# Query scaling on ScalarE, finer VectorE steps, moved loads and scatters, and expert pages in a written order, in a two-layer attention and mixture-of-experts kernel

## The chip, the cores and the metric

The kernel runs on one core of a Trainium2 chip. The core has five engines that run side by side, each with its own queue of instructions: TensorE (PE: matmuls and transposes; its weight loads are listed as PEld), VectorE (DVE), ScalarE (ACT), GpSimd (POOL), and SyncE (SP), which here only issues DMAs. POOL and ACT issue DMAs as well; the indirect ones (gathers and scatters by a list of rows) are issued by POOL. Engines wait for each other through semaphores, and an engine starts its instructions strictly in the order of its queue.

The metric is the device time of one execution in microseconds, smaller is better. An execution is taken as its span, from first to last instruction, and a small rest around it.

## The reference, cut to what matters

The input x is [4, 256, 256] in float32: 1,024 tokens of width 256. Four sublayers follow one another, each as x = x + layernorm(f(layernorm(x))).

```
# 1. attention over chunks of 32 tokens, 16 query heads, 4 key heads of 128
k = rms(xc @ w_k.T);  v = xc @ w_v.T;  q = rms(x @ w_q.T)        # rms over each head
scores = qr . landmark of each earlier chunk; 8 best; rw = softmax(scores)
p   = softmax over the 32 keys of each chosen chunk, times rw of the chunk
out = (p . v summed over chunks) @ w_o.T
# 2. mixture of 32 experts, 4 per token
logits = x @ gate_w.T + gate_b;  top 4, weights = softmax of the 4 logits
gate = min(xt @ w_gate + b_gate, 7);  up = clip(xt @ w_up + b_up, -7, 7)
o = ((up + 1) * gate * sigmoid(1.702 * gate)) @ w_down + b_down
y = sum over the 4 experts of o * weight
# 3. a gated scan over the 256 tokens of a row
lam = sigmoid(x @ W.T + b);  s = lam * s + (1 - lam) * x
# 4. a gated feed-forward layer with int8 weights, 256 -> 1024 -> 256
```

There are 8 chunks in a row of 256 tokens, so the best 8 are all the earlier chunks.

## The kernel before, in words

The program has three stages.

*Attention and routing* (us 0 to about 328 of the profile). The batch has four rows b of 256 tokens; a row is two tiles i of 128 tokens, so there are eight tiles. For each row the queries are made in 8 groups: a group is one tile and one key head kv, that is four query heads or 512 columns. One group goes: TensorE `pq` (L857); ScalarE squares each head and adds up (`jq`, L799, four instructions); VectorE `ssq` (L866) scales the sums; POOL `rq` (the helper `power`, L367) takes them to the power of minus one half; VectorE `qn` (L872) multiplies the four heads by it; TensorE turns them (`pqT`, L880), ScalarE copies them out (`qT`, L888). Keys go the same way (`pk` L808, `ssk` L814, `kn` L819, `pkT` L827, `kT` L831). Then come the scores (`s…` L957), a softmax per chunk in steps (`e…`: transpose and maximum on VectorE L900, subtraction on POOL L910, exponential on ScalarE L915, sums and inverse on VectorE, product), the products with v (`o…` L967, `att` L981) and the output matmul `wo` (L1005), one per tile.

Behind `wo` every tile is routed: the residual and two sets of statistics, the logits, the four best experts (`choose`), the rank of each token within its expert (`rank` L506), the slot (`rsl` L529) and the entries (`rent` L514) from which TensorE adds up the lists (`list` L539) that say which token stands in which row of which expert's page. From rank and expert VectorE also makes the rows (`places`) by which POOL scatters the normed token, once for each of its four experts, into `x_pages` in DRAM (L275): 32 scatters in all, four per tile.

The order of this stage is made when the program is built, by a list planner `Plan` (called `aplan`). Every step names its engine, an assumed cost, what it comes after, and the buffers that it takes and gives; a step whose chain to the end is the longest goes first, and a `lead` (LEAD for each later row) adds to the rank of the steps of the earlier rows. Steps named "D…" stand for the assumed arrival of loads (`arrival`). What the planner writes down is the order of instructions on every engine. At its end VectorE makes from the lists a gather list `gi` (L1115), and POOL's queue holds the scatters of tiles 4, 5 and 6, then the gathers, then the scatters of tile 7.

*Expert pages* (about 328 to 448). The 128 rows of one expert are a page; two pages go together (`pg` 0, 2 … 46: sixteen pairs for the 32 experts, then eight for rows that overflow a page). A pair goes: `page_fetch` (pages 0 to 7 by indirect gathers from `xn_dram` with gi, pages from 8 on read from x_pages by SP once all scatters have landed); `page_in` (transposes `px`, copy `pxT`); `page_up` (matmuls `pg` L1194 and L1199; VectorE `g` L1204 and `u` L1206; ScalarE sigmoid L1208; VectorE product L1209 and `h` L1211); `page_down` (transposes `ph` L1218, VectorE copy `hT` L1220, matmuls `po` L1224 and L1228, ScalarE copy `o` L1232, two scatters to `y_dram` by POOL, L1235). A `hook` adds side work between pairs: the lists of the overflow pages, the tables `mix` (L1406, L1408) for the sum over experts, the cast of the int8 weights (L1078). The order of instructions in this stage is left to the framework, which takes them as their inputs are due. The page's lists, weights and rows are read in `pages`, L1244 and on.

*Last layers* (448 to the end). `yk` (L1511) reads y_dram, TensorE sums the four experts with the tables mix (`y`, L1521), and the scan and the int8 layer follow under a second planner.

At the start POOL issues the loads of the gate and the biases (L331 to L338), fills the `att` tiles with zeros (L343), and then computes the small powers that the first tile waits for (L664 to L670, L367); SP issues x, the zero fill of x_pages and the expert weights.

## Time and profile before

| | us |
|---|---|
| median of 3 runs | 558.46 (557.94 to 558.66) |
| the profiled execution | 557.81 |
| its span | 556.0 |
| attention and the first seven tiles' routing, 16 to 285 | 269 |
| end of routing, 285 to 328 | 43 |
| pages, 328 to 448 | 120 |
| last layers, 448 to 556 | 108 |

The mean granted TensorE clock of the profiled execution is 0.934 of full speed. Its chain of work is 40% TensorE, 32% VectorE, 10% POOL, 7% issue, 5% ScalarE and 4% DMA.

The page gives the busy time of each engine over the whole span and then in slices; the table of stages gives the same for stretches that one chooses. A group line reads: source line, engine, operation, output and inputs by the program's names, shapes, count, then busy time, mean duration in ns, and the idle time of the engine just before these instructions with what ended it. A timeline line reads: start, duration, engine, source line, operation, and in brackets how long the engine had been idle before and what released it. Instructions of one engine overlap at their ends, so the distance from start to start is often shorter than the duration.

### The profile page before, as it was taken

The page shows a single profiled execution, that of the slowest core. Times are in us where ns is not written, and L with a number is a line of the kernel's source. Part 1 is how long each engine was busy: PE and PEld are TensorE (multiplying, and loading weights), DVE is VectorE, ACT ScalarE, POOL GpSimd, SP SyncE. Part 2 cuts the span into 40 slices and gives each one's busy share as a digit, 9 for nine tenths or more (in the row PEclk, how much of TensorE's full clock was granted, in tenths as well). Part 3 has the DMA queues.
Part 4 walks back from the last instruction along what each step waited for, and adds up shares of the span by engine and source line. Part 5 has one row for each costly group of instructions (what it writes and reads, how often), then busy time and mean ns, then how long its engine had stood idle before and what let it go on. Part 6 is the DMA issues. An engine that isn't in the chain of part 4 may idle for free.

```text
span 556.0 us, 7173 instructions
## 1 busy us (share of the span) xinstructions
PE 449.7 (81%) x1969; PEld 304.7 (55%) x1969; DVE 377.7 (68%) x1097; ACT 242.3 (44%) x762; POOL 313.0 (56%) x434
## 2 busy tenths in 40 slices
PE   0897988998979999888888227999999379589990
PEld 0353445664555565455666115888777258367760
DVE  3379997669897899999958944856444138853452
ACT  1674555534534545533220002336832117775541
POOL 6267676347446888436860774554554427845531
PEclk9999989999999999979999558999999879799996
DMA  8999999950000100003910584434957071000011
GB/s 255 360 386 369 349 348 348 349 189 1 9 1 21 38 10 28 2 28 99 365 57 9 161 308 129 131 118 145 367 175 243 23 260 45 1 0 1 1 40 38
DMA packets 59805, 80.68 MB, mean 145 GB/s; under 512 B 5684, under 2 KB 48682, under 8 KB 59760
## 3 DMA queue, kind: packets, MB, share of 16 engines
q1 hardware_dynamic: 54896, 70.33, 37.5%
q0 software_dynamic: 4576, 9.70, 5.1%
q10 hardware_dynamic: 288, 0.15, 0.2%
q8 instruction: 17, 0.28, 0.2%
q14 instruction: 28, 0.23, 0.1%
HBM read 37.16 MB, written 45.09 MB: 148 GB/s over the span
## 4 chain that ended last, share of the span: by engine, by line
PE 40%; DVE 32%; POOL 10%; issue 7%; ACT 5%; DMA 4%; another core or an unknown queue 1%; ACTq 0%; POOLq 0%; DVEq 0%; SPq 0%
PE pq L857 6%; PE pg L1199 5%; PE po L1228 3%; PE wo L1005 3%; PE y L1521 3%; PE u L1600 2%; PE d L1638 2%; PE g L1600 2%; POOL y_dram L1235 2%; PE pk L808 2%; DMA y_dram<-o,sib 1%; DMA gate_wT<-in_gate_wT 1%; PE px L1184 1%; DVE qn L872 1%; PE pqT L880 1%
## 5 line engine op out<-in xcount | busy, mean ns | idle before, releaser
L857 PE MATMUL pq<-w_q,xT 128*128 128x512 f32 x128 | 63.4, 619 | 3.6 <-DVE lm L733 1.3
L1005 PE MATMUL wo<-w_o,att 128*128 128x256 f32 x256 | 61.0, 382 | 3.9 <-DVE h L1025 3.9
L1005 PEld LDWEIGHTS wo<-w_o,att 128*128 128x128 f32 x256 | 47.3, 190 | 16.0 <-DVE h L1025 5.6
L1235 POOL DMA_INDIRECT y_dram<-o,sia x32 | 32.5, 1016 | 35.0 <-ACT o L1232 29.2
L799 ACT ACTIVATE jq<-pq 128x128 f32<-128x128 f32 x128 | 33.5, 275 | 28.3 <-PE pq L857 28.2
L367 POOL TENSOR_TENSOR rq<-ssq,mhalf 128x4 f32<-128x4 f32 x32 | 32.6, 1021 | 16.5 <-DVE ssq L866 16.1
L1204 DVE TENSOR_SCALAR g<-pg 128x256 f32<-128x256 f32 x24 | 10.2, 424 | 46.6 <-PE pg L1199 39.4
L857 PEld LDWEIGHTS pq<-w_q,xT 128*128 128x128 f32 x128 | 23.9, 197 | 27.4 <-issue 19.3
L275 POOL DMA_INDIRECT x_pages<-rxn,rowi x32 | 34.1, 1066 | 8.2 <-issue 6.8
L1199 PE MATMUL pg<-wexp,pxT 128*128 128x256 f32 x128 | 36.0, 395 | 0.2 <-issue 0.2
L1626 POOL TENSOR_TENSOR fl<-f,fh 128x512 fp32r<-128x512 f32 x15 | 19.2, 1290 | 23.4 <-ACT fh L1622 23.4
L1521 PE MATMUL y<-yk,mix 128*128 128x256 f32 x64 | 17.1, 417 | 11.9 <-DMA yk<-y_dram 11.2
L799 ACT ACTIVATION_READ_ACCUMULATOR jq<-pq 128x1 f32 x128 | 26.4, 206 | 0.0
L1232 ACT COPY o<-po 128x512 f32<-128x512 f32 x24 | 14.1, 585 | 27.4 <-PE po L1228 23.2
L1199 PEld LDWEIGHTS pg<-wexp,pxT 128*128 128x128 f32 x128 | 22.5, 198 | 4.3 <-issue 0.8
L1235 POOL DMA_INDIRECT y_dram<-o,sib x16 | 15.7, 984 | 16.0 <-ACT o L1232 13.2
L872 DVE TENSOR_TENSOR qn<-pq,rq 128x512 f32<-128x512 f32 x32 | 21.8, 680 | 4.2 <-POOL rq L367 2.3
L1615 DVE SCALAR_TENSOR_TENSOR f<-u,cols,sg 128x512 f32<-128x512 f32 x16 | 12.0, 750 | 18.4 <-PE u L1600 10.7
L888 ACT COPY qT<-pqT 128x512 f32<-128x512 f32 x32 | 18.8, 586 | 11.1 <-PE pqT L880 11.0
L880 PE MATMUL pqT<-ident,qn 128*128 128x128 f32 x128 | 20.2, 281 | 2.8 <-ACT qT L888 1.9
L880 PEld LDWEIGHTS pqT<-ident,qn 128*128 128x128 f32 x128 | 15.6, 146 | 10.4 <-issue 4.7
L1521 PEld LDWEIGHTS y<-yk,mix 128*128 128x128 f32 x64 | 12.9, 209 | 15.1 <-issue 11.6
(745 smaller groups left out, 1313.0 us busy)
## 6 DMA issues: line engine op xcount, KB each, us to landing
x_pages<-zeros SPq DMA_DIRECT2D x1, 31744.0 KB
wexp<-in_wcat SPq DMA_DIRECT2D x32, 384.0 KB
wov<-in_wcat SPq DMA_DIRECT2D x16, 384.0 KB
yk<-y_dram SPq DMA_DIRECT2D x8, 512.0 KB
xg<-x_pages SPq DMA_DIRECT2D x12, 256.0 KB
w_q<-in_wqT SPq DMA_DIRECT2D x4, 512.0 KB
w_o<-in_woT SPq DMA_DIRECT2D x2, 1024.0 KB
xg<-x_pages SPq DMA_DIRECT2D x16, 128.0 KB
```

The source lines that it names most:

```text
L275: nc.gpsimd.indirect_dma_start(out=x_views[i * TOPK + k], out_offset=IndirectOffsetOnAxis(ap=rowi[:, k : k + 1], axis=0), in_=xn, in_offse ...
L367: eng.tensor_tensor(dst, src, mhalf[:p, 0:1].to_broadcast([p, n]), ALU.pow)
L799: nc.scalar.activation(junk[:, 0:HD], src[:, ts(j, HD)], AF.Square, accum_out=dst[:, j : j + 1])
L857: nc.tensor.matmul(ps, keep[f"xT{b}"][:, k, ts(i, P)], wq[:, k, ts(kv, 512)], start=(k == 0), stop=(k == KD - 1))
L872: nc.vector.tensor_tensor(buf(p1, "qn", [P, G, HD], f"qn{n}"), keep[f"pq{n}"].rearrange("p (h d) -> p h d", h=G), rq[:, i, ts(kv, G)].unsq ...
L880: nc.tensor.transpose(ps[:, ts(j, P)], keep[f"qn{n}"][:, j, :], ident)
L1005: nc.tensor.matmul(keep[f"wo{b}{i}"][:, 0:D], keep[f"att{b}{kv}"][:, j, ts(i, P)], wo[:, kv * G + j, :], start=(kv == 0 and j == 0), stop= ...
L1199: nc.tensor.matmul(ps[:, j, :], xT[:, j, k, :], ws[j][:, ts(k, 2 * I)], start=False, stop=(k == KD - 1),)
L1235: nc.gpsimd.indirect_dma_start(out=y_views[pg + j], out_offset=IndirectOffsetOnAxis(ap=scl[:, q : q + 1], axis=0), in_=o[:, j, :], in_offs ...
L1521: nc.tensor.matmul(ps, mix[:, i * TOPK + k, :], keep[f"yk{i}"][:, k, :], start=(k == 0), stop=(k == TOPK - 1),)
L1600: nc.tensor.matmul(ps, ww[:, k, ts(o, P)], half[:, k, th], start=(k == 0 and j == 0), stop=(k == KD - 1 and j == 1),)
L1626: eng.tensor_tensor(buf("fl", [P, HALF], f"fl{n}{o}", F32R), keep[f"f{n}{o}"], keep[f"fh{n}{o}"].bitcast(F32), ALU.subtract,)
```

## The change

It has five parts.

1. *Scaling.* Queries and keys are multiplied by their inverse norms on ScalarE (`scaled_heads`, four instructions of 128 columns for each group, with the inverse norm as scale operand) in place of one VectorE product of 512 columns. The addition before the power moves from VectorE to POOL.
2. *Finer steps.* Steps that held several VectorE instructions (statistics, `choose`, `slots`, `places`, the softmax sums, the shares) become chains of single steps (`series`), which the planner can order one by one. The ranks are counted from the four one-hot tables with four matmuls, and no longer from their sum with one. Routing of the tiles of all rows but the last is given eight more units of rank (`sooner`), and LEAD is 20 and no longer 19; some assumed arrivals change.
3. *Loads and scatters.* The loads of gate and biases go from POOL's queue to SP's, the biases in one load (the host lays out `b_all`) and no longer nine; `g_pre` is issued before `cols`; the zero fill of att goes from POOL to VectorE. Scatters of tiles 4 and 5 are ordered like those before them; those of tile 6 are issued behind the first four page gathers, and those of tile 7 behind the next four.
4. *Pages in a written order.* `in_order` fixes the order of every engine as it is written: px of the next pair, ph and hT of the pair before, pg and h of this pair, po of the pair before, then the side work. `page_down` is split into `page_turn` (ph, hT) and `page_down` (po, o, scatters).
5. *Filling.* Matmuls without use are issued by TensorE: 6 at the start, 9 after the last list, 44 before `y`. The sigmoid is called once on one column after the last exponential.

```
+    g_pre = small("g_pre", [P, D])
     cols = small("cols", [P, 28])
-    g_pre = small("g_pre", [P, D])
...
+        nc.sync.dma_start(gate_w, t["gate_wT"].rearrange("(k p) n -> p k n", p=P))
+        nc.sync.dma_start(gate_b, t["gate_b"].to_broadcast([P, E]))
+        nc.sync.dma_start(brow, t["b_all"])
...
-            nc.gpsimd.memset(a[:, :, 0:S], 0.0)
+            nc.vector.memset(a[:, :, 0:S], 0.0)
...
+        def series(add, eng, after, *links, take=(), give=(), lead=None):
+            more = {} if lead is None else {"lead": lead}
+            for n, (cost, emit) in enumerate(links):
+                after = [add(eng, cost, after, emit, take=take if n == 0 else (),
+                             give=give if n == len(links) - 1 else (), **more)]
+            return after[0]
...
+            def scaled_heads(dst, src, by):
+                for j in range(by.shape[1]):
+                    nc.scalar.activation(
+                        dst[:, j, :], src[:, ts(j, HD)], AF.Copy, scale=by[:, j : j + 1])
...
-                        nc.vector.tensor_scalar(q, q, c_h[:, i : i + 1], None, ALU.add)
-                    a = add("V", 0.13, [a, sc1], sum_q)
+                        nc.gpsimd.tensor_scalar(q, q, c_h[:, i : i + 1], None, ALU.add)
+                        power(rq[:, i, ts(kv, G)], q)
+                    a = add("P", 1.3, [a, sc1], norm_q)
...
-                        nc.vector.tensor_tensor(
-                            buf(p1, "qn", [P, G, HD], f"qn{n}"),
-                            keep[f"pq{n}"].rearrange("p (h d) -> p h d", h=G),
-                            rq[:, i, ts(kv, G)].unsqueeze(2).to_broadcast([P, G, HD]), ALU.mult)
-                    a = add("V", 0.6, [a, turns.get("qn")], scale_q, take=["qn"], give=["mm"])
+                        scaled_heads(buf(p1, "qn", [P, G, HD], f"qn{n}"), keep[f"pq{n}"],
+                                     rq[:, i, ts(kv, G)])
+                    a = add("A", 0.66, [a, turns.get("qn")], scale_q, take=["qn"], give=["mm"])
...
-                nc.tensor.matmul(pr, before, keep[f"rchosen{i}"], start=False, stop=True)
+                for k in range(TOPK):
+                    nc.tensor.matmul(
+                        pr, before, pick[:, k0 + k, :], start=False, stop=(k == TOPK - 1))
...
-                routing(2 * b + i, b, a, add)
+                routing(2 * b + i, b, a, add if b == B - 1 else sooner)
...
+        with tc.issue_after(keep["listed"].ins):
+            warm(9, flat(ps_o.tile([P, 2, D], F32, tag="o", name="warm2")))
...
+            ordered = in_order()
+            ahead = []
+            for n, pg in enumerate(pgs[:4]):
+                ahead.append(page_fetch(pg))
+                if pgs[0] == 0 and n % 2:
+                    for k in range(TOPK):
+                        scatter_token(TT - 2 + n // 2, k, *last_scatter[n // 2])
+                ordered()
...
                 if n + 1 < len(pgs):
                     nxt = page_in(pgs[n + 1], ahead.pop(0))
+                    ordered()
+                if pend is not None:
+                    pend = page_turn(*pend)
+                    ordered()
                 h = page_up(pg, xT, ws)
+                ordered()
                 if pend is not None:
                     page_down(*pend)
+                    ordered()
                 pend = (pg, h, ws)
                 if hook is not None:
                     hook(pg)
-            page_down(*pend)
+                    ordered()
+            page_down(*page_turn(*pend))
...
-        plan.run(limits, in_order())
+        ordered = in_order()
+        warm(44, ps_l1.tile([P, HALF], F32, tag="d", name="warm3", bufs=2))
+        ordered()
+        plan.run(limits, ordered)
```

## The prediction

> **What bounds the kernel now.** I read the page's totals first, then the table of stages, the groups of ScalarE and VectorE in the attention stage, the waits of TensorE there, and last the timelines of the three places where the change moves DMA issues. Totals and the clock over 40 slices:
>
> ```profile
> PE 449.7 (81%) x1969; PEld 304.7 (55%) x1969; DVE 377.7 (68%) x1097; ACT 242.3 (44%) x762; POOL 313.0 (56%) x434
> ...
> PEclk9999989999999999979999558999999879799996
> ```
>
> TensorE is busy most of the time, but 81% is an average over stages with different limits. By stage (window, its length, then busy time of PE, PEld, DVE, ACT, POOL, clock):
>
> ```profile
> 16.00:40.00 24.00, 22.64 (x76) 11.34 (x76) 12.14 (x41) 18.13 (x88) 12.73 (x17) 1.00 1.09 375
> 40.00:285.00 245.00, 219.43 (x857) 134.35 (x857) 212.93 (x572) 112.20 (x426) 156.07 (x188) 0.97 0.44 150
> 285.00:328.00 43.00, 23.23 (x123) 17.61 (x122) 32.20 (x144) 3.60 (x11) 20.73 (x29) 0.77 0.40 134
> ...
> 345.00:436.00 91.00, 88.14 (x514) 69.83 (x514) 53.89 (x146) 42.25 (x93) 44.32 (x44) 0.98 0.56 191
> 436.00:448.00 12.00, 1.10 (x5) 0.55 (x5) 0.41 (x1) 0.58 (x1) 3.94 (x4) 0.72 0.20 65
> ```
>
> Attention (16 to 285): TensorE 242 of 269 us, VectorE 225, ScalarE 130. TensorE is nearly full and VectorE is the next limit. The end of routing (285 to 328) is serial. The pages (345 to 436) are TensorE's, 88 of 91 us, and the 12 us behind them are a wait for a DMA. In attention the largest single gaps of TensorE stand after VectorE: rank after qn 4.2 us, wo after h 3.9, xq after qn 1.7, s02x after e01x 1.7, list after rsl 1.5, pq after lm 1.3, rwx0p after sel 1.2, together 15.5; after ScalarE 7.2 (o10x and o01x after att 2.5 and 1.7, pqT after qT 1.9, pq after v 1.1). The groups that the change touches there (busy us, mean ns | idle before):
>
> ```profile
> L799 ACT ACTIVATE jq<-pq 128x128 f32<-128x128 f32 x128 | 33.5, 275 | 28.3 <-PE pq L857 28.2
> L872 DVE TENSOR_TENSOR qn<-pq,rq 128x512 f32<-128x512 f32 x32 | 21.8, 680 | 4.2 <-POOL rq L367 2.3 <-PE pqT L880 1.9
> L866 DVE TENSOR_SCALAR ssq<-ssq,c_h 128x4 f32<-128x4 f32 x32 | 8.9, 281 | 7.4 <-ACT jq L799 7.4
> ```
>
> **The change, part by part.**
>
> *Start.* Before, POOL issues eleven gate and bias loads of 0.50 us each, then the att memset, and only then the small power that the first `xs` waits for:
>
> ```profile
> 10.27 0.50 POOL L336 DMA_DIRECT2D brow<-in_b_gate  x1 [3.78 <-DMA gate_wT<-in_gate_wT]
> ...
> 14.29 0.48 DVE L638 SCALAR_TENSOR_TENSOR xs<-x_all,mv,g_pre 128x256 f32<-128x256 f32 x1
> ```
>
> After, POOL has none of these; the loads go to SP's queue behind the four x loads and ahead of the zero fill and the expert weights, whose readers come tens of us later (the bias from 60 us on). x is there at 3.7 us, `cols` at 3.0, and `g_pre` at 6.6, now issued first. `xs` can start at about 7.3, psx at 8.2, and the first query matmul at 9.3 to 9.8 where it was 16.40: **−6.6 us** (5.5 to 8). The memsets go to VectorE (0.80 us there, in its idle start); the six warming matmuls stand before psx on an idle TensorE: nothing, as long as x and g_pre land after they end.
>
> *Scaling on ScalarE.* VectorE loses 32 `qn` of 0.680 (21.8), 8 `kn` of 0.681 (5.5), 32 `ssq` of 0.281 (8.9) and 8 `ssk`: about 38 us. The sums go to POOL, 40 × 0.2 (rows L664 to L670: 0.19 to 0.24) = 8 us, beside 169 of 269. Each group of four heads becomes four ScalarE instructions of 128×128 with a scale operand, 160 in all. No row is exactly this. Lower bound: ACTIVATE L799 to the start of its accumulator read, 0.17. Upper bound: L1408, 128×128 with a scale operand, three in a row in 1.00, 0.29 start to start. Worked out between: copies of 512 and 256 columns take 586 and 378, so 128 columns 274 ns; a scale operand adds 0.1 (kT L831 699 against 586), a back-to-back instruction overlaps by 0.1 (L1078: two in 1.14, one in 0.62). I take 0.26, nearest to L1408, which has the same form: 1.05 us a group, 42 us in all (27 to 48). ScalarE goes from 130 to 172 of 269 (64%), VectorE from 225 to 187 (70%).
>
> The Trainium skill, "ScalarE: Activation LUTs", section "Rules for kernel authors", speaks against this move: multiplication belongs on VectorE, not on ScalarE. By the figures of its section "What ACT_TABLE_LOAD costs" (186 ns + 0.833 ns a column, 93 more for a pointer operand, 93 less back to back) I estimate 0.29 per instruction, 47 us in all; by that the sum would come out 1 us higher, in the early window alone.
>
> What it is worth: a 680 ns instruction becomes a 1.05 us one on the chain of every query group, but groups are worked ahead by several, so only queues count. In the first 24 us ScalarE is already at 18.1, and eight groups there need 8.4 more: 26.5 in 24 us. So part of the early start is given back: **+4 us** (a hand-made chain puts the copy of the second query block at 37 where it was 40.8, a lead of 3 instead of 6.6). From 40 on TensorE idles 26 of 245 us; 15.5 us of gaps stand after VectorE. Splitting long VectorE steps (choose 1.25 us, slots 1.0, softmax sums) lets urgent small ones pass, routing of the first six tiles gets priority, and the last batch's wo matmuls run between its heads, not after them: 6.5 us of TensorE work are left behind the last att transposes where there were 19. I take half of the 26 us of idle as regained: **−12 us**. Ends: 0, if ScalarE takes VectorE's place as the one that comes last, and −25, if TensorE fills up. 24 more rank matmuls are bf16 with 32 columns and cost about 0.1 us each, 2 us within this.
>
> *Gathers before scatters.* From the last wo to the gather list `gi` I count the same 15.5 us in both orders of VectorE (ten small steps now stand before gi, but tiles 4 and 5 are out of the way). The list is there at 319.5, but POOL has a backlog of scatters, about 1.27 apart, before the first gather:
>
> ```profile
> 318.01 0.96 POOL L275 DMA_INDIRECT x_pages<-rxn,rowi  x1 [0.30 <-issue]
> ...
> 326.03 1.75 POOL L1163 DMA_INDIRECT xg<-xn_dram,gi  x1 [0.30 <-issue]
> ```
>
> After, tiles 4 and 5 scatter earlier, and the eight of tiles 6 and 7 stand behind four gathers each: the first gather starts right after gi, **−6.3 us**. Pages from 8 on read x_pages and wait for the last scatter. That one stays eight gathers and sixteen issues behind the list, as before, and moves with it. The read of page 8 was issued at 343.75 and pages 0 to 6 need about 27 us, so it is no later than they are.
>
> *Pages in a written order.* Before, one page pair takes 3.83 us of TensorE without a gap, and the transposes of h come late enough to have h at hand (VectorE, pg at 391.03):
>
> ```profile
> 392.10 0.42 DVE L1204 TENSOR_SCALAR g<-pg 128x256 f32<-128x256 f32 x1 [1.66 <-PE pg L1199]
> 392.44 0.41 DVE L1206 TENSOR_SCALAR u<-pg 128x256 f32<-128x256 f32 x1
> ...
> 393.48 0.42 DVE L1209 TENSOR_TENSOR g<-g,sg 128x256 f32<-128x256 f32 x1 [0.30 <-ACT mix L1408]
> 393.94 0.43 DVE L1211 SCALAR_TENSOR_TENSOR h<-u,g 128x256 f32<-128x256 f32 x1
> ```
>
> h ends 2.3 us after pg does. In the new order TensorE has po of the page before (1.08) and px of the next (0.43) between pg(n) and ph(n): 1.5 us against 2.2, a stall of 0.6 to 0.7. Period: 2.14 + 0.22 + 1.95 (pg) = 4.3. Between h(n) and hT(n) VectorE also has the side work of the page (bias lists, mix tiles), written there, and for pages 4 to 10 I come to 4.6 to 5.6. From the first gather to g of page 46 that makes 115.5 against 106.7 us: +8.8. The overflow pages stay at about 4.25. The end is shorter, since po follows its page by one and not two: last scatter 6.1 us after the last pg, before 7.4: −1.3. Together **+7.5 us** (0, if the unexplained 5.5 us wait of VectorE at 338.4 goes; +14 if every page has the side work in its way). ScalarE's table load (1.28 us, before the first sigmoid) comes earlier, within these bounds.
>
> *The 44 warming matmuls* before y. In the pages the 96×256 bf16 matmuls issue 0.11 apart, so a 128×512 one takes about 0.22 and all 9.5 us; the wait for yk is 11.19:
>
> ```profile
> 448.29 4.04 PE L1521 MATMUL y<-yk,mix 128*128 128x256 f32 x10 [11.19 <-DMA yk<-y_dram]
> ```
>
> They fit, and y, which ran at 0.40 each, runs at 0.22 from the start: **−2 us** (0 to −2.5). If they ran at half clock (0.43 each, 19 us) they would hold y up by 8; they follow a busy TensorE (clock 0.98 in the pages), so I take them as fast. The six at the start are counted at nothing: had they raised the clock, the first four pq would take 1.9 us and not the 3.78 that they show behind the cold psx. The Trainium skill, "TensorE: Matmul & The Clock Gate", Part 1, wants a busy window of about 3.4 us before the clock rises; by it, six of 0.43 us are too few, and the sum stays; without that rule it would be 1.9 lower.
>
> **Sum.** −6.6 + 4 − 12 − 6.3 + 7.5 − 2 = −15.4 us. The profiled execution took 557.8 (span 556.0 and 1.8 around it), 0.65 below the median of the runs: 542.4 against it, 543 as a median.
>
> **Rivals.**
> 1. *TensorE fills up* (likelier if the queue of VectorE was behind most gaps, as 15.5 of 23 us say; against it, ScalarE gets 42 us): body −22 to −25, 531.
> 2. *ScalarE takes VectorE's place*: 0.29 each, 48 us, and the square sums of the next group stand behind the scaling of the last in its queue; body 0: 555. For it, ScalarE's 26.5 in the first 24 us; against it, 36% idle later.
> 3. *The other side: the written order of the pages.* Place: ph behind h, with side work on VectorE between. Mean period from g of page 0 to g of page 46: before 4.19, forecast 4.61. Each 0.1 us costs 2.3 us. All else gives −22.9, the short end −1.3: slower from 5.25 us a page on. At 5.6, the upper end of my chain for pages with side work, +32: 566. Against it: only seven pages have much of it. The same side is reached if rival 2 and a period of 4.9 meet.
>
> **How the numbers follow.** Chances: forecast 0.48 (its own range 535 to 551), rival 1 0.17, rival 2 0.17, rival 3 0.12, and mixtures that end about where it was 0.06. A measurement of this kernel tells about 0.2% (1.1 us) from no change. Faster 0.81, within 0.03, slower 0.16. The range reaches from rival 1's lower side to the time before: 526 to 559.
>
> **What would show it.** First pq near 9.5 us; VectorE near 187 and ScalarE near 172 us in attention, TensorE above 93% there; first gather within 1 us of gi and no scatters between; TensorE waiting 0.6 us for h in every page; y at 0.22 each. Wrong if attention's TensorE share stays at 90%, if ScalarE is named as releaser of most gaps, if pages take over 5 us, or if the 44 matmuls end after yk lands.

## The result and the profile after

The changed kernel takes 553.8 us (median of 7 runs, 552.1 to 556.9) against 558.5 (7 runs, 557.9 to 559.8): a ratio of 0.9916, with a 95% interval of 0.9889 to 0.9944. It is 4.7 us faster. The forecast was 543, 15.4 us faster: the direction and the range (526 to 559) hold, but the gain is less than a third of what was forecast.

The totals of the page of the changed kernel (columns as before), and the TensorE clock by slices:

```profile
span 551.0 us, 7443 instructions
...
PE 465.7 (85%) x2050; PEld 308.6 (56%) x2052; DVE 341.4 (62%) x1015; ACT 283.1 (51%) x923; POOL 327.0 (59%) x466
...
PEclk9999999999999998998996679999999899689997
```

ScalarE is busy for 41 us more and VectorE for 36 less, as the scaling moved. TensorE has 16 more, nearly all of it filling matmuls. The table of stages (window, length, busy PE, PEld, DVE, ACT, POOL, clock):

```profile
16.00:40.00 24.00, 20.11 (x79) 10.39 (x78) 8.03 (x32) 23.22 (x113) 17.23 (x30) 1.00 1.09 371
40.00:265.00 225.00, 208.30 (x860) 128.93 (x859) 171.18 (x503) 138.86 (x545) 166.93 (x221) 0.98 0.46 156
265.00:305.00 40.00, 30.00 (x131) 21.46 (x132) 29.00 (x102) 9.55 (x19) 17.81 (x27) 0.86 0.32 115
305.00:317.00 12.00, 8.32 (x26) 4.39 (x23) 0.35 (x2) 1.39 (x4) 8.91 (x9) 0.64 0.56 210
317.00:329.00 12.00, 7.83 (x30) 5.51 (x30) 5.07 (x22) 1.34 (x4) 6.83 (x7) 0.67 0.30 94
...
345.00:433.00 88.00, 75.70 (x446) 57.87 (x444) 49.58 (x126) 38.84 (x84) 42.11 (x41) 1.00 0.54 172
433.00:445.00 12.00, 10.66 (x42) 4.61 (x44) 0.00 (x0) 0.00 (x0) 0.99 (x1) 0.86 0.50 172
```

From 16 to 40 ScalarE is busy for 23.2 of 24 us. The pages, where TensorE was 97% busy before, are at 86%: it now waits in nearly every pair. In the 12 us before y it is busy, and where it waited for a DMA before, y now waits for TensorE itself. Five points in time, read off the timelines of the two profiles, divide the 5.0 us between the spans:

| stretch | before | after | change | forecast |
|---|---|---|---|---|
| start to first gather of pages | 326.0 | 305.4 | −20.6 | −20.9 |
| first gather to g of page 46 | 106.7 | 121.2 | +14.5 | +8.8 |
| g of page 46 to last scatter to y_dram | 7.15 | 6.4 | −0.75 | −1.3 |
| last scatter to y | 8.4 | 12.25 | +3.85 | 0 |
| y to the end | 107.7 | 105.7 | −2.0 | −2 |

So the front came as forecast, and all of the miss lies behind the first gather.

### The profile page after: what moved, and what is told of

Same layout as the page of the kernel before. It is cut to its first block, busy times and chain, and to the rows that moved or that the text cites. A ratio compares the mean times of both kernels' runs of the same rounds, so it can differ in the third digit from the quotient of the medians.

```text
span 551.0 us, 7443 instructions
## 1 busy us (share of the span) xinstructions
PE 465.7 (85%) x2050; PEld 308.6 (56%) x2052; DVE 341.4 (62%) x1015; ACT 283.1 (51%) x923; POOL 327.0 (59%) x466
## 5 line engine op out<-in xcount | busy, mean ns | idle before, releaser
L1292 POOL DMA_INDIRECT y_dram<-o,sia x32 | 34.7, 1084 | 39.6 <-ACT o L1289 34.7
L844 ACT ACTIVATE qn<-pq,rq 128x128 f32<-128x128 f32 x128 | 36.9, 382 | 9.8 <-POOL rq L380 8.8
L1262 ACT ACTIVATE sg<-g 128x256 f32<-128x256 f32 x24 | 10.0, 417 | 60.7 <-DVE g L1258 54.3
L1258 DVE TENSOR_SCALAR g<-pg 128x256 f32<-128x256 f32 x24 | 10.2, 424 | 41.4 <-issue 12.2
L1698 POOL TENSOR_TENSOR fl<-f,fh 128x512 fp32r<-128x512 f32 x15 | 19.3, 1292 | 23.9 <-ACT fh L1694 23.9
L839 ACT ACTIVATION_READ_ACCUMULATOR jq<-pq 128x1 f32 x128 | 27.7, 219 | 0.0
L1253 PEld LDWEIGHTS pg<-wexp,pxT 128*128 128x128 f32 x128 | 23.9, 208 | 4.8 <-issue 0.6
L160 PE MATMUL warm<-pick,ones_b 128*128 128x512 bf16 x57 | 17.6, 470 | 6.8 <-issue 3.6
L919 PEld LDWEIGHTS pqT<-ident,qn 128*128 128x128 f32 x128 | 15.6, 143 | 11.8 <-issue 5.9
L1271 PE MATMUL ph<-ident,h 128*128 128x128 f32 x48 | 10.0, 291 | 13.5 <-DVE h L1265 10.2
L909 POOL TENSOR_SCALAR ssq<-ssq,c_h 128x4 f32<-128x4 f32 x32 | 11.1, 348 | 16.5 <-ACT jq L839 16.2
```

The source lines that it names most:

```text
L160: last = nc.tensor.matmul(ps, ones_b, flat(pick)[:, 0:512], start=True, stop=True)
L839: nc.scalar.activation(junk[:, 0:HD], src[:, ts(j, HD)], AF.Square, accum_out=dst[:, j : j + 1])
L844: nc.scalar.activation(dst[:, j, :], src[:, ts(j, HD)], AF.Copy, scale=by[:, j : j + 1])
L919: nc.tensor.transpose(ps[:, ts(j, P)], keep[f"qn{n}"][:, j, :], ident)
L1253: nc.tensor.matmul(ps[:, j, :], xT[:, j, k, :], ws[j][:, ts(k, 2 * I)], start=False, stop=(k == KD - 1),)
L1292: nc.gpsimd.indirect_dma_start(out=y_views[pg + j], out_offset=IndirectOffsetOnAxis(ap=scl[:, q : q + 1], axis=0), in_=o[:, j, :], in_offs ...
```

## The experiments

Each kernel changes the changed kernel (called "after" below) in the place that its diff shows; best1 to best3 join several such edits. The times are medians; the ratio is to the kernel before, run beside it. There are six sets of runs, and the last five were each taken on a chip of their own (the column "chip"; that of the first set is not on record). The kernel before takes 558.5 to 560.6 us in them, so a difference of 1 or 2 us between runs of different chips says little.

| run | chip | what is different | us | ratio (95%) | first gather | first gather to g of page 46 | last scatter to y |
|---|---|---|---|---|---|---|---|
| after | ? | | 553.8 | 0.992 (0.989 to 0.994) | 305.4 | 121.2 | 12.3 |
| again | 10 | the same once more | 554.6 | 0.989 (0.985 to 0.994) | 306.6 | 121.8 | 12.2 |
| w24 | 7 | 24 filling matmuls before y | 546.4 | 0.977 (0.975 to 0.980) | 307.3 | 118.1 | 8.0 |
| w40 | 11 | 40 of them | 548.4 | 0.979 (0.976 to 0.982) | 306.1 | 118.2 | 11.4 |
| w0 | 11 | none | 547.2 | 0.978 (0.975 to 0.981) | 305.8 | 117.9 | 7.9 |
| free | 7 | page order left to the framework | 540.9 | 0.966 (0.963 to 0.969) | 307.7 | 110.7 | 9.8 |
| pxlate | 10 | px behind pg | 553.3 | 0.987 (0.982 to 0.992) | 305.7 | 121.8 | 12.2 |
| gfirst | 10 | eight gathers, then the scatters | 555.7 | 0.993 (0.989 to 0.996) | 305.9 | 123.2 | 12.9 |
| w18 | 4 | 18 filling matmuls after the last list | 553.2 | 0.990 (0.986 to 0.993) | 305.0 | 121.1 | 12.4 |
| lag | 7 | po two pairs behind | 560.2 | 1.002 (1.000 to 1.004) | 307.1 | 131.4 | 8.4 |
| vscale | 7 | scaling on VectorE | 541.8 | 0.968 (0.966 to 0.971) | 297.6 | 118.6 | 11.8 |
| vplan | 12 | scaling on VectorE, planned as ScalarE's | 549.5 | 0.981 (0.979 to 0.983) | 306.8 | 118.2 | 11.5 |
| acost | 12 | planner told 1.2 us a group | 546.2 | 0.975 (0.973 to 0.978) | 302.6 | 118.0 | 12.3 |
| nostart | 10 | the start of the kernel before | 558.8 | 0.998 (0.995 to 1.000) | 309.2 | 123.8 | 12.9 |
| best1 | 12 | vscale, free, w24 | 532.9 | 0.952 (0.949 to 0.954) | 296.3 | 111.4 | 7.8 |
| best2 | 12 | vscale, w24, lag for the first 32 pages | 531.0 | 0.949 (0.947 to 0.951) | 296.3 | 110.6 | 7.9 |
| best3 | 4 | best2 and w18 | 540.0 | 0.965 (0.961 to 0.969) | 296.7 | 119.2 | 9.6 |

### The matmuls before y: w24, w40, w0

```
-        warm(44, ps_l1.tile([P, HALF], F32, tag="d", name="warm3", bufs=2))
+        warm(24, ps_l1.tile([P, HALF], F32, tag="d", name="warm3", bufs=2))
```

> Only edit: 24 filling matmuls before y where the changed kernel has 44. Theory: the 44 start 3.7 us after the last po (the branch behind the pages lies between), the first seven run at half clock, and they end at 445.4, about 4 us after yk could be there (8.4 us after the last scatter, as in the kernel before, is 441.4). With 24 they end near 441, y starts 3 to 4 us earlier and still runs at 0.22 each: 549 to 550.5 us against 553.8. Rival: y waits for yk anyway, which lands near 445: y starts where it did, and the time stays within 1 us.

The timeline of all engines in the changed kernel, before y:

```profile
434.12 0.58 PE L160 MATMUL warm<-pick,ones_b 128*128 128x512 bf16 x1 [3.33 <-issue]
434.93 10.51 PE L160 MATMUL warm<-pick,ones_b 128*128 128x512 bf16 x42 [0.22 <-issue]
...
437.58 1.97 SPq L1583 DMA_DIRECT2D yk<-y_dram  x4
...
445.27 1.89 PE L1593 MATMUL y<-yk,mix 128*128 128x256 f32 x8
```

and TensorE's of w24:

```profile
432.85 0.58 PE L160 MATMUL warm<-pick,ones_b 128*128 128x512 bf16 x1 [3.36 <-issue]
433.65 6.19 PE L160 MATMUL warm<-pick,ones_b 128*128 128x512 bf16 x22 [0.22 <-issue]
439.68 3.62 PE L1593 MATMUL y<-yk,mix 128*128 128x256 f32 x16
```

The matmuls start 3.3 us after the last po. A branch of the program lies between the pages and the last layers; how much of the 3.3 us it takes is not shown (in best1 and best2, with the same branch, it is 1.0). The first seven run 0.43 apart, the others 0.213, and y follows them without a gap. In w24 y comes 8.0 us after the last scatter, and in after 12.25: the 44 hold y back by 4.3 us. The rival, that yk is late anyway, falls. Most of the rest of the 7.4 us by which w24 is faster is another matter (below).

```
-        warm(44, ps_l1.tile([P, HALF], F32, tag="d", name="warm3", bufs=2))
```

> Only edit: no filling matmuls before y. If they are worth anything, y runs at half clock here (0.40 to 0.45 each for the first 16 as in the kernel before) and starts at 8.0 to 8.4 us after the last scatter: 2 us above w24 in the stretch from there to the end, 4 minus 2 us below the changed kernel there. With or without the gap of VectorE: 548.5 or 552 us. Rival (the fill costs and brings nothing): as fast as w24 from y on, 546.

Without them (w0, next fence) y waits for its DMA and comes 7.9 us after the last scatter, no sooner than in w24:

```profile
437.99 5.34 PE L1593 MATMUL y<-yk,mix 128*128 128x256 f32 x16 [10.14 <-DMA yk<-y_dram]
```

Sixteen matmuls take 5.34 us and not 3.62; from y to the end it is 106.75 us in w0 and 105.06 in w24. So the clock is worth 1.7 us, about as forecast, and in w24 the 24 filling matmuls bring it. The medians, from two chips, hardly tell the two apart (547.2 and 546.4, ratios 0.978 and 0.977), and the number 24 does not carry over to best1 and best2 (see there).

### The order of the pages: free, lag, pxlate, gfirst

```
...
                     nxt = page_in(pgs[n + 1], ahead.pop(0))
-                    ordered()
-                if pend is not None:
-                    pend = page_turn(*pend)
-                    ordered()
                 h = page_up(pg, xT, ws)
-                ordered()
                 if pend is not None:
-                    page_down(*pend)
+                    page_down(*page_turn(*pend))
...
```

> Only edit: the order of the page stage is left to the framework again (the gathers and scatters in front of it stay as written). Theory: the written order costs the pages 0.6 us each, by TensorE waiting for h, and holds the second pair back behind the transposes of the third, whose gathers stand behind four scatters: from the first gather to g of page 46 it takes 121.2 us, and would take about 107 again with the free order, so about 540 to 543 us. Rival: the pages are slow because of where the gathers and scatters stand and because of the low clock at their start; then the free order gives 115 us or more and 548 us or more.

Measured 540.9: 12.9 us less in the medians. First gather to the last g takes 110.7 us where it took 121.2 (the theory said 107). But w24, which has the written order and ran on the same chip as free, takes 118.1: so 7.4 us are the price of the written order. Of the rest, 3.1 are a gap of VectorE that after has and w24 has not (below), and 2.4 are the filling, which holds y back by less here. The steady pairs of the changed kernel on TensorE and VectorE:

```profile
424.58 1.03 PE L1253 MATMUL pg<-wov,pxT 128*128 128x256 f32 x4
425.55 1.03 PE L1253 MATMUL pg<-wov,pxT 128*128 128x256 f32 x4
...
426.53 0.60 PE L1285 MATMUL po<-wov,hT 128*128 128x256 f32 x2
427.08 0.60 PE L1285 MATMUL po<-wov,hT 128*128 128x256 f32 x2
428.62 0.41 PE L1271 MATMUL ph<-ident,h 128*128 128x128 f32 x2 [0.95 <-DVE h L1265]
```

po ends, and ph waits for h. In pairs that still have a next px it waits 0.5 to 0.6 us, and g comes every 4.40 us (404.62, 409.02, 413.42 …) where it was 3.83.

The body of the loop in lag, without its calls of `ordered()`:

```
                 h = page_up(pg, xT, ws)
                 if n + 1 < len(pgs):
                     nxt = page_in(pgs[n + 1], ahead.pop(0))
                 if pend is not None:
                     turned = page_turn(*pend)
                 if down is not None:
                     page_down(*down)      # po of two pairs before
                 down = turned
```

> Only edit: still a written order, but pg of a pair first, then px of the next, ph of the pair before and po of the pair two before, so that TensorE never comes to ph before h is made, nor to the third pair's transposes before pg of the second. Theory of the stall: period 3.8 to 3.9 us where it was 4.4, second pair about 4 us sooner, the whole from first gather to g of page 46 about 107 us, at the end 1 us more for the last po: 542 to 545 us. Rival (a written order as such is slow, or the DMAs set the pace): period stays above 4.2 us, 550 us or more.

Missed, at 560.2. In the second half of the first 32 pages most pairs come every 3.65 to 3.84 us, as the theory of the stall says, and no ph waits for its h any more; the overflow pages then take 8 to 9.5 (g on VectorE in lag):

```profile
390.20 0.42 DVE L1258 TENSOR_SCALAR g<-pg 128x256 f32<-128x256 f32 x1 [1.51 <-PE pg L1253]
393.90 0.42 DVE L1258 TENSOR_SCALAR g<-pg 128x256 f32<-128x256 f32 x1 [1.51 <-PE pg L1253]
402.77 0.42 DVE L1258 TENSOR_SCALAR g<-pg 128x256 f32<-128x256 f32 x1 [6.68 <-PE pg L1253]
412.22 0.42 DVE L1258 TENSOR_SCALAR g<-pg 128x256 f32<-128x256 f32 x1 [7.27 <-PE pg L1253]
```

These read their weights into six buffers, and a pair holds two of them one step longer. In the trace pg waits there for the load of its weights (2.46 us in front of the matmul at 398.18, 2.22 in front of that at 408.15); that the buffers make the load late is argued, not shown. best2, which lags in the first 32 pages alone, has 4.4 us in the overflow pages. So the rival in its broad form falls: a written order as such is not slow, the distance from h to ph is what costs.

```
-                if n + 1 < len(pgs):
-                    nxt = page_in(pgs[n + 1], ahead.pop(0))
                 if pend is not None:
                     pend = page_turn(*pend)
                 h = page_up(pg, xT, ws)
+                if n + 1 < len(pgs):
+                    nxt = page_in(pgs[n + 1], ahead.pop(0))
```

> Only edit: the transposes px of the next pair are written behind pg of this pair, not before ph. Theory (px of the third pair holds pg of the second up until its gathers land): g of the second pair 1.5 to 2.5 us sooner after g of the first, the period of 4.40 unchanged since ph still waits for h; time 1.5 to 3 us below the changed kernel's. Rival (the second pair is late because of the half clock and h alone): the same time within 1 us.

```
-                if pgs[0] == 0 and n % 2:
-                    for k in range(TOPK):
-                        scatter_token(TT - 2 + n // 2, k, *last_scatter[n // 2])
...
+            if pgs[0] == 0:
+                for m in range(2):
+                    for k in range(TOPK):
+                        scatter_token(TT - 2 + m, k, *last_scatter[m])
```

> Only edit: all eight page gathers are issued first, and the scatters of tiles 6 and 7 behind them. Theory (the gathers of the third and fourth pairs, 5.1 us late behind four scatters, hold the first pairs up): they land 5 us sooner, g of the second pair 1 to 2 us sooner, time 1 to 2.5 us below the changed kernel's, the last scatter where it was. Rival (they are not what is waited for): the same within 1 us.

Both take the time of after within the spread (553.3 and 555.7; after has 553.8, and 554.6 as again on their chip), so in the time neither theory gains. In pxlate g of the second pair comes 8.25 us after the first and not 11.5, but the third comes 8.6 after the second (4.35 in after). In gfirst pg of the second pair starts at 318.3, where after has 321.0, and yet its g comes at 328.5: VectorE does not start it, with pg done at 320.3. The wait for the gathers is real, but a gap on VectorE that ends no earlier covers it, and so neither run can price it.

### The gap of VectorE: again, w40, w18, best3

> The changed kernel itself, beside the three below. Its first runs lay between 552.1 and 556.9, wider than those of any other kernel here, and the second pair of pages came 11.5 us after the first in its profile, 9.0 to 9.1 us in all experiments with the same page code. If that was chance of the execution, this run gives 549 to 552 us and 9 us; if it belongs to the kernel, 553 to 556 and above 11.

```
-        warm(44, ps_l1.tile([P, HALF], F32, tag="d", name="warm3", bufs=2))
+        warm(40, ps_l1.tile([P, HALF], F32, tag="d", name="warm3", bufs=2))
```

> Only edit: 40 filling matmuls before y for 44, all of it behind the pages. By the count alone y comes 0.9 us earlier (four of 0.213): 553 us. In some kernels (the changed one, w18, best3, the kernel before) VectorE idles 3 to 9 us in front of g of the second pair, with pg done and no wait shown, and goes on when the last scatter of tokens has been issued; in w24, which differs from the changed kernel behind the pages only, it does not. Theory L (where the instructions lie in memory decides, not what they do): a change behind the pages alone can make the gap come or go here, too: 553 with the gap, 549 to 550 without it. Rival (the gap is a matter of the work ahead of it): it is there, as in the changed kernel's two profiles.

In after, pg of the second pair is done at 324.8, VectorE has nothing ahead of g, and still g starts 3.4 us later. The timeline of all engines in after:

```profile
321.54 0.41 DVE L1273 COPY hT<-ph 128x256 f32<-128x256 f32 x1
...
322.90 1.91 PE L1253 MATMUL pg<-wexp,pxT 128*128 128x256 f32 x4
...
324.77 0.97 POOL L282 DMA_INDIRECT x_pages<-rxn,rowi  x1 [0.30 <-issue]
...
327.73 0.94 SPq L1198 DMA_DIRECT2D xg<-x_pages  x2
328.20 0.42 DVE L1258 TENSOR_SCALAR g<-pg 128x256 f32<-128x256 f32 x1 [6.26 <-PE px L1238]
```

and w24, with the same code in this place:

```profile
322.90 0.42 DVE L1273 COPY hT<-ph 128x256 f32<-128x256 f32 x1
...
324.79 1.91 PE L1253 MATMUL pg<-wexp,pxT 128*128 128x256 f32 x4
...
326.74 0.42 DVE L1258 TENSOR_SCALAR g<-pg 128x256 f32<-128x256 f32 x1 [3.42 <-PE pg L1253]
```

The same gap stands in the profile of the kernel before (g of the second pair comes 4.8 us after its pg), in again (2.3), pxlate (3.0), gfirst (7.0), nostart (3.4), w18 (3.3) and best3 (7.4). It is in none of w24, w40, w0, free, lag, vscale, vplan, acost, best1 and best2. It costs about 3 us: with the page code of after, first gather to the last g takes 121.1 to 123.8 us where the gap is (after, again, w18, nostart) and 117.9 to 118.6 where it is not (w24, w40, w0, vscale, vplan, acost).

w24, w40 and w0 differ from after behind the pages only, as theory L wants it. But the record holds a rival that the expectations do not name, the chip:

| chip | kernels | gap | updates of TensorE's semaphore in the trace, of those expected | kernel before, us |
|---|---|---|---|---|
| ? | before, after | in both | 449 of 477, 419 of 452 | 558.5 |
| 7 | w24, free, lag, vscale | in none | all | 559.0 |
| 12 | best1, best2, acost, vplan | in none | all | 560.0 |
| 10 | again, pxlate, gfirst, nostart | in all | 416 to 421 of 452 | 559.8 |
| 4 | w18, best3 | in both | 422 of 452, 421 of 449 | 559.8 |
| 11 | w40, w0 | in none | all | 560.6 |

The gap goes with the set of runs, and so with the chip, in all 18 profiles. As far as the chips are on record, no kernel was run both on a chip with the gap and on one without. So neither theory L nor its rival, the work ahead of the gap, is decided: where the gap came or went, the set of runs changed together with the program. w40 came without the gap and near the 549 to 550 us that theory L gave for that case, but the chip tells the same. again shows only that the gap came back in a second set. Against a plain effect of the chip speaks the kernel before, which has the gap in its one profile and yet is no faster on the chips where the others have none. w24 or after on each other's chip would tell; no such run is on record.

The traces also show what VectorE waits for. g starts when the count of TensorE's semaphore is reached, and the packed trace has the times of its updates. In w24 an update is there at 326.72, 0.02 us after the end of pg, and g starts at 326.74. In after TensorE ends pg, po, prow and px between 324.8 and 327.0, but the next four updates stand at 328.18, 328.26, 328.32 and 328.38, and g starts 0.02 us behind the first. In before, gfirst, nostart and w18 g starts behind the first of such a late burst, too. In again and pxlate a single late update frees it and the burst comes 0.8 and 4.3 us behind that; in best3 the update that frees g is missing, and the burst comes 2.2 us behind g. None of the ten profiles without a gap has a late update (but for the end of the program). In the kernel before the burst frees VectorE and, 0.1 us later, ScalarE, whose px had ended at 339.5:

```profile
338.87 0.60 PE L1184 MATMUL px<-ident,xg 128*128 128x128 f32 x4
...
343.85 0.42 DVE L1204 TENSOR_SCALAR g<-pg 128x256 f32<-128x256 f32 x1 [5.48 <-remote]
343.96 0.58 ACT L1186 COPY pxT<-px 128x512 f32<-128x512 f32 x1 [2.78 <-remote]
```

So VectorE is not slow there: it waits for the signal of TensorE, which comes late. In these same profiles some 6 to 8% of the updates of that semaphore are missing from the trace. What delays the signals, and whether the gap is there when no trace is taken, no run shows. In five of the eight the gap ends 0.1 to 0.5 us after SP could issue its read of page 8, that is when the last scatter of tokens has landed (327.73 and 328.20 in after), but in again, best3 and pxlate 0.5, 1.8 and 4.1 us ahead of that.

```
-            warm(9, flat(ps_o.tile([P, 2, D], F32, tag="o", name="warm2")))
+            warm(18, flat(ps_o.tile([P, 2, D], F32, tag="o", name="warm2")))
```

> Only edit: 18 filling matmuls after the last list where the changed kernel has 9. In the changed kernel's profile the nine end 2.5 us before the first page's transposes, and the first two pairs' pg still take 1.91 us per four (1.03 later). Theory H (the half clock is a term of the first three pairs' 4 us over the forecast): with 18 the clock is up at the first pg, the first pairs save 2 to 3.5 us, 550.5 to 552.5 us. Rival (these pairs wait for gathers and for VectorE whatever the clock): pg is faster but g of the third pair comes within 1 us of where it came, and the time stays within 1 us.

With nine, the first pg ran at half clock (two times 1.91 us in after). With 18 (timeline of TensorE in w18):

```profile
303.15 6.14 PE L160 MATMUL warm<-pick,ones_b 128*128 128x512 bf16 x18 [0.44 <-DVE lists L582]
...
312.18 1.03 PE L1253 MATMUL pg<-wexp,pxT 128*128 128x256 f32 x4
313.16 1.03 PE L1253 MATMUL pg<-wexp,pxT 128*128 128x256 f32 x4
...
318.18 0.66 PE L1238 MATMUL px<-ident,xg 128*128 128x128 f32 x2 [3.98 <-DMA xg<-xn_dram,gi]
...
320.52 1.91 PE L1253 MATMUL pg<-wexp,pxT 128*128 128x256 f32 x4
```

The first pair is fast, and the 2 us are spent again: px of the third pair waits for its gather, TensorE idles for 4 us, and the clock is down for the second pair. Its pg is done 19.3 us after the first gather, in after 19.4, and the gap of VectorE follows in both. The rival is right: 553.2 us. The Trainium skill, "TensorE: Matmul & The Clock Gate", Part 1, gives about 3.4 us both for the busy window that raises the clock and for the idle one that lowers it. This trace agrees with the idle one (granted clock 1.00 up to 317.6 and 0.50 from 317.7 on, 3.5 us into the idle stretch of 4.0). The trace of after does not: there, too, the clock rose at the end of the nine, to 1.00 from 307.8 to 311.2, and was back at 0.50 from 311.2 to 324.8, though TensorE had idled for only 2.5 us (307.6 to 310.1) and been busy for 0.9 us since.

> The fastest so far (scaling on VectorE, po two pairs behind, 24 matmuls before y) with 18 matmuls after the last list where it has 9. Theory H: 2 to 3 us less than 531.0, so 528 to 529. Rival: within 1 us of 531, as the third pair waits for its gathers there, too.

best3 is 9 us slower than best2, which neither theory says: the gap of VectorE, absent in best2, is 7.4 us there (pg ends at 308.1, VectorE's side work at 309.7, and g starts at 317.1). As best2 ran on chip 12 and best3 on chip 4, this cannot be put down to the edit alone.

### The scaling: vscale, vplan, acost

In vscale and vplan the queries and keys are scaled by one VectorE product; in vplan the planner is still told that it is ScalarE's work.

```
-                for j in range(by.shape[1]):
-                    nc.scalar.activation(
-                        dst[:, j, :], src[:, ts(j, HD)], AF.Copy, scale=by[:, j : j + 1])
+                n = by.shape[1]
+                nc.vector.tensor_tensor(
+                    dst, src.rearrange("p (h d) -> p h d", h=n),
+                    by.unsqueeze(2).to_broadcast([P, n, HD]), ALU.mult)
...
-                    a = add("A", 0.66, [a, turns.get("qn")], scale_q, take=["qn"], give=["mm"])
+                    a = add("V", 0.6, [a, turns.get("qn")], scale_q, take=["qn"], give=["mm"])
```

> Only edit: queries and keys are scaled by one VectorE product per group again; everything else, the finer steps and the planner's costs for the step included, as in the changed kernel. Theory (VectorE was the next limit in attention, and relieving it is half of the gain there): the first gather comes 4 to 8 us later than 305.4, the time is 558 to 562. Rival 1 (finer steps and the order of routing make the gain, the scaling nothing): first gather within 1.5 us, time within 2 us. Rival 2 (ScalarE is now what comes last in the first 40 us): first gather earlier, 549 to 552.

The theory is refuted with its sign: 541.8 us, and the first gather at 297.6, where the ten kernels whose attention stage is that of after have 305.0 to 307.7 (the three on the same chip 307.1 to 307.7). The scaling on ScalarE is a loss of some 7 to 10 us. The instructions cost what the upper bound said (groups of after; 36.9 us in 128 qn is 0.288 each). The estimate of 0.29 that the prediction worked out from the Trainium skill, "ScalarE: Activation LUTs", section "What ACT_TABLE_LOAD costs", agrees with the second of these rows (the sum took 0.26):

```profile
L839 ACT ACTIVATE jq<-pq 128x128 f32<-128x128 f32 x128 | 33.9, 288 | 27.3 <-PE pq L900 27.1
L844 ACT ACTIVATE qn<-pq,rq 128x128 f32<-128x128 f32 x128 | 36.9, 382 | 9.8 <-POOL rq L380 8.8
```

But where is it lost? The same stretches, first of after, then of vscale:

```profile
16.00:40.00 24.00, 20.11 (x79) 10.39 (x78) 8.03 (x32) 23.22 (x113) 17.23 (x30) 1.00 1.09 371
...
240.00:280.00 40.00, 32.15 (x128) 20.00 (x127) 39.10 (x102) 18.55 (x53) 32.83 (x36) 0.91 0.50 184
```

```profile
16.00:40.00 24.00, 23.42 (x91) 11.89 (x90) 15.34 (x48) 19.29 (x98) 20.15 (x32) 1.00 1.09 372
...
240.00:280.00 40.00, 35.05 (x137) 22.27 (x136) 32.47 (x80) 14.74 (x34) 28.77 (x32) 0.96 0.49 178
```

From 16 to 40 TensorE works 3.3 us less beside a full ScalarE. From 240 to 280 it works 2.9 us less beside a VectorE that is busy for 39 of 40 us: VectorE has less to do in all, but more of it late. Which of the two is the cause, ScalarE's time or the plan that it leads to, the next two ask.

```
-                    nc.scalar.activation(
-                        dst[:, j, :], src[:, ts(j, HD)], AF.Copy, scale=by[:, j : j + 1])
+                nc.vector.tensor_tensor(
+                    dst, src.rearrange("p (h d) -> p h d", h=n),
+                    by.unsqueeze(2).to_broadcast([P, n, HD]), ALU.mult)
...
                     a = add("A", 0.66, [a, turns.get("qn")], scale_q, take=["qn"], give=["mm"])
```

> Scaling executed on VectorE, but planned as ScalarE's, at 0.66: the order of all other instructions is that of the changed kernel. Theory E (ScalarE's time is what costs): most of the 8 to 10 us by which the first gather came earlier with VectorE's own plan comes here too: first gather at 297 to 300, 541 to 546 us. Theory M (the plan's order costs): first gather at 303 or later, 549 us or more.

```
-                    a = add("A", 0.66, [a, turns.get("qn")], scale_q, take=["qn"], give=["mm"])
+                    a = add("A", 1.2, [a, turns.get("qn")], scale_q, take=["qn"], give=["mm"])
```

> Only edit: the planner is told 1.2 us for a group's scaling on ScalarE (four instructions of 0.29 as measured) where it was told 0.66. Theory M (the loss by the scaling comes from a plan made with too low a cost, which puts ScalarE's work and what hangs on it too late): the first gather comes 3 to 8 us earlier than 305.4 to 307, time 545 to 550. Theory E (ScalarE has no room in the first 40 us and its chains get longer whatever the plan): first gather within 2 us, 552 to 556.

vplan, with the scaling back on VectorE but the changed kernel's order, has its first gather at 306.8: the 7 to 10 us are gone. So taking the work off ScalarE brings nothing without an order that is made for it, as theory M has it. It does not clear ScalarE's time as a cause, since in vplan VectorE has some 27 us of products (40 of 0.68) that its order does not reckon with, which may cost as much as they save. acost, where the planner is told a price near the measured one (four of 0.29), brings the first gather to 302.6, 2.4 to 5.0 us before the ten. So that much of the loss is the order that the too low price of 0.66 led to. The other 5 us (6.3 against best1 and best2 on the same chip) remain with ScalarE's scaling at a nearly true price. That they come from a ScalarE that is still full early on (22.75 us busy of 24 from 16 to 40, 34.75 of 40 from 40 to 80 in acost) is argued, not shown. The medians of vscale, vplan and acost hold 3 us more gain that is not the scaling's, since their pages have no gap of VectorE.

### The start, and the best version: nostart, best1, best2

```
...
+        nc.gpsimd.dma_start(gate_w, t["gate_wT"].rearrange("(k p) n -> p k n", p=P))
+        nc.gpsimd.dma_start(gate_b, t["gate_b"].to_broadcast([P, E]))
+        for j in range(3):
+            for c in ((0, I), (I, 2 * I), (2 * I, 2 * I + D)):
+                nc.gpsimd.dma_start(brow[ts(j, E), c[0] : c[1]], t["b_all"][ts(j, E), c[0] : c[1]])
...
-            nc.vector.memset(a[:, :, 0:S], 0.0)
+            nc.gpsimd.memset(a[:, :, 0:S], 0.0)
```

> Only edit: the start as in the kernel before: gate and bias loads (eleven issues) and the att memsets on POOL, cols ahead of g_pre. Theory (start gains 5.5 us, of which ScalarE in the first 40 us gives 4 back): first pq near 16 us, first gather 1 to 3 us later than the changed kernel's. Rival (all of the start arrives): first gather 5 to 6 us later.

First pq at 15.78 us, where after has it at 10.89 and the three others on this chip at 10.5 to 10.7; first gather at 309.2, that is 2.6 to 3.5 later than theirs. So the start gains about 5 us at the first matmul, and some 2 of them are lost again before the first gather; that this is where ScalarE is full is argued, not shown. The total is 558.8, 4.2 us above again and 5.0 above after.

> Three edits to the changed kernel together: scaling on VectorE, the framework's own order in the page stage, 24 filling matmuls. If the three losses are separate places (attention, pages, the wait for yk), they add up: 12.0 for the scaling, 12.9 for the order (which alone leaves y waiting for yk, so part of the matmuls' loss is in it), 0 to 4 for the matmuls: 527 to 531 us. If they share a cause, the sum falls short: 534 or more.

> Scaling on VectorE, 24 filling matmuls, and a written page order with po two pairs behind for the first 32 pages and as in the changed kernel for the overflow pages. Theory: the lag alone lost in the overflow pages (9 us a pair, weights held for longer than there are buffers) and won before them (3.7 us a pair against 4.4); with the overflow pages at 4.4 the pages take about 109 us from the first gather to the last g, and the time is 526 to 532 us. Rival (the overflow pages lose with any written order): more than 5 us a pair there, 535 us or more.

best1 comes out at 532.9, 2 to 6 us above what the sum of separate places gave, so the gains overlap: the 3 us of the gap, absent on the chips of vscale and free, are counted in both, and the filling brings nothing here. TensorE starts it 1.0 us after the last po, it ends 4.2 us ahead of yk, and y finds a low clock; its first sixteen matmuls take 6.6 us (3.6 in w24):

```profile
413.09 5.39 PE L160 MATMUL warm<-pick,ones_b 128*128 128x512 bf16 x23 [1.01 <-ACTq L1473]
422.65 7.71 PE L1584 MATMUL y<-yk,mix 128*128 128x256 f32 x21 [4.17 <-DMA yk<-y_dram]
```

In best2 the same happens after 2.3 us of idle time (5.4 us for sixteen). From y to the end best1 takes 107.8 us and best2 107.1, so by the 105.1 of w24 a count that fits would bring them 2 to 3 us, by estimate. best2 is the fastest, 531.0 us, 29.0 below the kernel before beside it (ratio 0.949, 0.947 to 0.951) and 23 below the changed kernel. Some of its pages on VectorE:

```profile
347.04 0.42 DVE L1259 TENSOR_SCALAR g<-pg 128x256 f32<-128x256 f32 x1 [0.93 <-PE pg L1254]
350.74 0.42 DVE L1259 TENSOR_SCALAR g<-pg 128x256 f32<-128x256 f32 x1 [1.51 <-PE pg L1254]
354.44 0.42 DVE L1259 TENSOR_SCALAR g<-pg 128x256 f32<-128x256 f32 x1 [1.51 <-PE pg L1254]
```

A pair every 3.70 us there, less than the 3.83 of the kernel before. Over the whole stretch best2 is not better: 110.6 us from the first gather to the last g against 106.7, with 7.9 us from the second pair's g to the third's and 4.3 to 4.4 in the overflow pages. Its gain lies ahead of the pages.

## Why the prediction was right or wrong

The forecast was −15.4 us and the spans differ by −5.0. Of the 10.4 us between, 0.3 lie ahead of the first gather, 6.3 in the pages and 3.9 at the matmuls before y.

*Up to the first gather: right in the sum, and partly for a wrong reason.* Start −5.5 (forecast −6.6): psx came at 8.08, as forecast, and the first pq then waited 1.6 us for ScalarE's copy of it. From the first pq to the last wo 281.0 us for 287.6, −6.6 (forecast +4 and −12). From the last wo to gi 12.4 for 15.5, −3.1 (forecast 0). From gi to the first gather 1.2 for 6.6, −5.4 (forecast −6.3); the timelines of VectorE and POOL show it:

```profile
304.26 0.18 DVE L1169 SCALAR_TENSOR_TENSOR gi<-lists 128x32 uint32<-128x32 f32 x1
...
305.44 1.11 POOL L1217 DMA_INDIRECT xg<-xn_dram,gi  x1 [8.02 <-DMA wexp<-in_wcat]
306.86 0.96 POOL L1217 DMA_INDIRECT xg<-xn_dram,gi  x1 [0.30 <-issue]
```

What was wrong inside: "VectorE is the next limit" was taken as a reason for a gain from moving the scaling. vscale shows that this part costs 7 to 10 us, and what remains, the finer steps, the order of routing, the start and the gathers, gains about 28 (326.0 to 297.6). The sign for the scaling was wrong, and the sum hid it: that the stretch came out right is in part luck. The step that failed there is "groups are worked ahead by several, so only queues count". The planner's order hangs on the price that it is told, which the prediction did not look at, though both prices (0.66 planned, 1.05 worked out) were at hand; acost puts 2.4 to 5.0 us on it, and what causes the other 5 stays open.

*Pages: the term that was mis-sized.* Forecast +7.5, measured +13.75 (+14.5 and −0.75). The mechanism, ph waiting for h, is right with its size: 4.40 a pair (forecast 4.3), and 0.5 to 0.6 us of wait (forecast 0.6 to 0.7). But the wait comes in nearly every pair: 4.40 us holds in the overflow pages, too, which the prediction kept at 4.25. The rest is at the front. First gather to g of page 6 was put at about 27 us and took 31.5; from there to page 46 it took 89.6 for 88.5. Of these 5.7 us, about 3 are the gap of VectorE (121.2 against 117.9 to 118.2 in w24, w40 and w0, from other sets), which the prediction met in the kernel before as "the unexplained 5.5 us wait" and treated as something that could only go. What causes it stays open. The other 2.6 stand where the first pairs run at half clock and the third pair's gathers wait behind four scatters. The prediction counted neither in its price of the pages; that these two make up the 2.6 is argued, and w18 shows that the clock of the first pair alone brings nothing.

*The matmuls before y: the step "they fit" failed.* Forecast −2, measured +1.85 (y 3.85 later, and 2.0 less behind it). Their number at full clock was priced correctly, 0.213 each. What was left out is when they can start, and how: TensorE idles 3.3 us in front of them, starts late and starts at half clock. Started at the end of the last po (430.8) and 0.213 apart, 44 would have ended at about 440.2, ahead of yk (8.0 us after the last scatter, 441.0); they ended at 445.4. The runs with 24, 40 and 44 of them have y 8.0, 11.4 and 12.3 us after the last scatter. The prediction had the clock in view ("if they ran at half clock") and dismissed it, since "they follow a busy TensorE"; the profile of before had the same stretch empty, behind the last po, and its 11.19 us of idle were read as all of it being free to fill. The wait that counts runs to yk, 8 us after the last scatter and 4 us before the end of the filling.

*Rivals.* None of the three came. Rival 3 named the right place, and its price for 0.1 us a pair was right; at 4.78 us a pair from first to last g it stayed below its point of 5.25. Rival 2 was closer than it seemed: ScalarE's scaling loses time and brings none.

*What would show it* was useful as written: the first gather came 1.2 us after gi, the wait for h stands in nearly every pair, and one sign of being wrong, "if the 44 matmuls end after yk lands", is what happened. Another nearly did: from 16 to 285 VectorE is busy for 196 us (forecast 187) and ScalarE for 168 (172), but TensorE for 246 of 269, 91%, where above 93% was to show the forecast and 90% to refute it.

## What to carry to other kernels

Work that is put into an engine's idle time is priced from when that engine can start it, past branches and at the clock that it finds, to the moment when the awaited thing lands: not by the length of the idle row. A count that fits one kernel (24 in w24) does not fit the next (best1), where the engine starts sooner. Moving work to a less busy engine can lose when a planner orders everything by assumed prices; telling the planner the measured price (acost) shows a part of that, and is cheap to run. A term that comes out right in the sum may hold two errors: undoing one part at a time showed a loss of 7 to 10 us inside a gain of 21. And two kernels that run on two chips differ in two things: run both on the same chip before a difference is put down to the edit.

## What was not expected of the hardware

A gap of 2 to 7 us on VectorE before g of the second pair of pages stands in all eight profiles from three sets of runs and in none of the ten from the three others. It comes with late updates of TensorE's semaphore, three or four within 0.2 us, and with updates that are missing from the trace. Whether the chip, the program or the taking of the trace brings it is open. While it is, a difference of 1% between two versions of this kernel from different sets says little about the edit between them unless this stretch is compared first.
